# Local attention scores with keys on the partitions, and the softmax sums made across them

## The chip, the cores and the metric

The kernel runs on one core of one Trainium2 chip. The metric is the device time of one execution, in microseconds. Of three timed runs of the kernel before, the median is 2884.61 us, with 2884.58 us as the lowest and 2886.78 us as the highest. The core has five engines that work side by side, each on its own instruction queue in its own order: TensorE (PE, matrix products and transposes; its weight loads are listed apart as PEld), VectorE (DVE), ScalarE (ACT), GpSimd (POOL), and SyncE (SP), which here only issues loads. Matrix products land in a small memory of their own, PSUM; everything else is in SBUF.

## The reference

The input is x of shape (8, 1024, 512) in float32: 8 batches of 1024 tokens. Cut to what matters:

```python
xn = layernorm(x)
q, k, v = split(xn @ local_qkv_w, 3)                      # head size 128
local_out  = softmax(q @ k.T * scale) @ v                 # all 1024 keys
sparse_out = softmax(top-k of (q @ k.T * scale)) @ v      # own weights, k = 102
mem_out    = (softmax(p @ bank.T) @ bank, with p) @ ...   # a memory of 64 rows
pred_out   = two layers with an exact gelu
s = concat(local_out, sparse_out, mem_out, pred_out) @ warboss_w + warboss_b
g = silu(relu(xn @ w1 + b1) @ w2 + b2)                    # 512 -> 2048 -> 512
out = x + s * g
```

The change touches `local_out` alone: the scores of each query against all 1024 keys, the softmax over the keys (largest value subtracted, exponential, division by the sum), and the product with v.

## The kernel before

**Tiling.** A batch has 8 tiles of 128 tokens (`NT`), taken as 4 pairs of 256 tokens (`NP`, `T` = 256). A tile of queries is the unit of the two attentions, a pair is the unit of everything behind them. Over the 8 batches there are 64 tiles and 32 pairs.

**Local attention of one tile** (`local`, line 823). `scores` makes two products of 128 queries by 512 keys, with queries on the partitions, and ACT copies them from PSUM into the tile `el` (128x1024). DVE takes the negated maximum of each row (`nml`, a reduction along the row). ACT forms the exponentials in place with that maximum as its bias and sums them along the row in the same instruction. `normalize` (line 785) takes the reciprocal of the sum on DVE and multiplies the row by it on ACT. `transpose_probs` (line 794) turns the eight 128x128 blocks of probabilities on PE, since the product with v needs the keys on the partitions, and ACT copies the turned blocks to `pT0`. After the second tile of a pair `attend` (line 807) multiplies all 8 chunks of v with `pT0` into the head, 128 channels by 256 queries.

**Sparse attention of one tile** (`sparse`, `sparse_select`) is the same, but its selection takes DVE 13 rounds: eight largest values (MAX8), then their replacement (MATCH_REPLACE8), then the threshold applied in one SCALAR_TENSOR_TENSOR. This is most of DVE's work and is strictly in order.

**The rest.** The feed-forward products, and those of q, k, the memory and the output, are made by a scheme that replaces eight block products by seven and pays with block sums. The sums of PE's results (`add_products`, tiles `u_up`, `u_po`, `m`) and those of its operands (`left_sums`, tile `hs`) are POOL's work; without `hs` PE cannot go on with the second layer of the feed-forward part.

**What sets the order.** Nothing reacts at run time: the program is written out by a planner while it is built. It keeps a clock per engine in units of PE columns (`tick`, `on`, `after`, lines 115 to 128), in which a product of 256 columns counts 256 and a transposition 64. Each piece of work is a generator (a chain) that is put forward again when its due time has come by PE's clock; in between, PE's order is filled with feed-forward products (`feed_forward`, line 665) whenever these are due. `after("dve", 200)` means: go on when DVE should have finished by the planner's price, plus 200 columns. `SLACK` is 400 columns. DVE's rounds of the sparse selection are put into DVE's order whenever DVE's clock falls behind PE's. `pool_is_free` (line 509) holds a POOL instruction back until POOL's planned backlog is under 300 columns. The wrapper `InOrder` (line 79) then fixes each engine's order to the planner's. A new tile is begun every `STEP` columns (line 1076). So the planner's prices decide in which order instructions stand, and on the chip an instruction whose input is late holds up everything behind it on its engine.

All instructions pass through that wrapper, so the profile gives line 85 for almost every one; they are told apart by the names of their tiles.

Of the kernel before, what the change touches and what calls it, by code (L numbers as in the profile page):

```python
# [9 lines left out]
F32 = mybir.dt.float32  # L10
AF = mybir.ActivationFunctionType
ALU = mybir.AluOpType
AX = mybir.AxisListType
PSUM = bass.MemoryType.PSUM

P = 128
# [4 lines left out]
def kernel(  # L21
# [25 lines left out]
    B, S, D = x.shape  # L47
# [4 lines left out]
    NT = S // P  # L52
    NP = NT // 2
    NG = NT // 4
    T = 2 * P
# [3 lines left out]
    NWC = NW // WC  # L59
# [4 lines left out]
    LOCAL, SPARSE = 0, 1  # L64

    const = ctx.enter_context(tc.tile_pool(name="const", bufs=1))
    sb = ctx.enter_context(tc.tile_pool(name="sb", bufs=1))
    small = ctx.enter_context(tc.tile_pool(name="small", bufs=2))
# [8 lines left out]
    class InOrder:  # L77
# [23 lines left out]
    pe, act, dve, pool, sp = (  # L101
        InOrder(e) for e in (nc.tensor, nc.scalar, nc.vector, nc.gpsimd, nc.sync)
    )
# [11 lines left out]
    def tick(columns):  # L115
        clock["pe"] += columns
        while rounds and clock["dve"] < clock["pe"]:
            cost = next(rounds[0], None)
            if cost is None:
                rounds.pop(0)  # L120
            else:
                clock["dve"] = max(clock["dve"], clock["pe"] - 1600) + cost

    def on(engine, columns):
        clock[engine] = max(clock[engine], clock["pe"]) + columns

    def after(engine, more=SLACK):
        return clock[engine] + more
# [29 lines left out]
    def start(generator, due=0, rank=1):  # L158
        chains.append([due, generator, rank])
        chains.sort(key=lambda c: c[2])  # L160

    def matmul(out, lhsT, rhs, start, stop, columns):
        pe.matmul(out, lhsT, rhs, start=start, stop=stop)
        tick(columns)

    def transpose(out, in_, ident):
        pe.transpose(out, in_, ident)
        tick(P // 2)
# [6 lines left out]
    def copy(out, ps, columns):  # L175
        act.copy(out, ps)
        on("act", columns)

    def on_pool(op, out, in0, in1):
        getattr(pool, op)(out, in0, in1)  # L180
        n = 1
        for d in out.shape[1:]:
            n *= d
        on("pool", 60 + int(1.42 * n))
# [5 lines left out]
    def ring(name, shape):  # L190
        return ps_r.tile(list(shape), F32, tag="r", name=name)


    ident = const.tile([P, P], F32, tag="ident", name="ident")
# [35 lines left out]
    for h in range(2):  # L230
        t = sb.tile([P, 2, D], F32, tag="s", name=f"xl_0_{h}", bufs=2)
# [14 lines left out]
    for v in (ffn_b1, mem_out_b, pred_in_b, pred1_b, pred2_b):  # L246
        n = v.shape[0] // P
# [37 lines left out]
    done = set()  # L285
    stats = {}
    xnT = {}
    qT = {}
    kT = {}
    vv = {}  # L290

    def needs(*keys):
        return lambda: all(k in done for k in keys)
# [102 lines left out]
    H = D // 2  # L396
# [376 lines left out]
    probsT = {}  # L773
    heads = {}

    def scores(b, i, h, s):

        for c in range(S // 512):
            ps = ring(f"sc_{b}_{i}_{h}_{c}", (P, 512))
            matmul(  # L780
                ps, qT[b, i // 2][:, h, ts(i % 2, P)], kT[b][:, h, ts(c, 512)], True, True, 512
            )
            copy(s[:, ts(c, 512)], ps, 360)

    def normalize(e, total, name):
        r = small.tile([P, 1], F32, tag="r", name=f"r_{name}", bufs=4)
        dve.reciprocal(r, total)
        on("dve", 100)
        yield after("dve", 100)
        act.activation(e, e, AF.Copy, scale=r)  # L790
        on("act", 690)
        yield after("act")

    def transpose_probs(b, i, h, e):
        if i % 2 == 0:
            if (b, i) != (0, 0):
                yield needs(("head", *divmod(b * NP + i // 2 - 1, NP), h))
            probsT[b, i // 2, h] = sb.tile([P, NT, T], F32, tag=f"pT{h}", name=f"pT_{b}_{i}_{h}")
        for c in range(NT // 4):
            pt = ring(f"ptp_{b}_{i}_{h}_{c}", (P, 4, P))  # L800
            for k in range(4):
                transpose(pt[:, k, :], e[:, ts(4 * c + k, P)], ident)
            copy(probsT[b, i // 2, h][:, ts(c, 4), ts(i % 2, P)], pt, 360)
            yield clock["pe"] + 300
        done.add(("pT", b, i, h))

    def attend(b, p, h):
        ps = ring(f"pa_{b}_{p}_{h}", (P, T))
        accumulate(
            ps,  # L810
            [vv[b][:, k, h, :] for k in range(NT)],
            [probsT[b, p, h][:, k, :] for k in range(NT)],
            T,
        )
        o = sb.tile([P, T], F32, tag=f"head{h}", name=f"head_{b}_{p}_{h}")
        copy(o, ps, 220)
        heads[b, p, h] = o
        done.add(("head", b, p, h))

    def before_pair(b, p):  # L820
        return [] if (b, p) == (0, 0) else [("joined", *divmod(b * NP + p - 1, NP))]

    def local(b, i):
        yield needs(("q", b, i // 2), *[("k", b, g, LOCAL) for g in range(NG)])
        yield after("act", 0)
        if (b, i) != (0, 0):
            yield needs(("pT", *divmod(b * NT + i - 1, NT), LOCAL))
        e = sb.tile([P, S], F32, tag="el", name=f"el_{b}_{i}")
        scores(b, i, LOCAL, e)
        done.add(("local scores", b, i))  # L830
        yield after("act")
        nm = small.tile([P, 1], F32, tag="nm", name=f"nml_{b}_{i}", bufs=4)
        dve.tensor_reduce(nm, e, AX.X, ALU.max, negate=True)
        on("dve", 740)
        yield after("dve", 100)
        total = small.tile([P, 1], F32, tag="total", name=f"totl_{b}_{i}", bufs=4)
        act.activation(e, e, AF.Exp, bias=nm, accum_out=total)
        on("act", 800)
        yield after("act", 100)
        yield from normalize(e, total, f"l_{b}_{i}")  # L840
        yield from transpose_probs(b, i, LOCAL, e)
        if i % 2:
            yield needs(("v", b), *before_pair(b, i // 2))
            yield after("act")
            attend(b, i // 2, LOCAL)
        done.add(("local", b, i))

    def sparse_scores(b, i):
        s = sb.tile([P, S], F32, tag="s", name=f"s_{b}_{i}", bufs=2)
# [38 lines left out]
    def sparse(b, i):  # L888
        n = b * NT + i
        yield needs(("q", b, i // 2), *[("k", b, g, SPARSE) for g in range(NG)])  # L890
        if n > 1:
            yield needs(("chosen", n - 2))
        yield max(clock["pe"], clock["act"]) + (SLACK if n else 100)
        s = sparse_scores(b, i)
        done.add(("sparse scores", n))
        yield after("act")
        o = {}
        rounds.append(sparse_select(b, i, s, o))
        yield lambda: "nm" in o
        if n:  # L900
            yield needs(("pT", *divmod(n - 1, NT), SPARSE))
        e = sb.tile([P, S], F32, tag="es", name=f"es_{b}_{i}")
        act.activation(e, s, AF.Exp, bias=o["nm"])
        on("act", 700)
        o["e"] = e
        yield lambda: "total" in o
        done.add(("chosen", n))
        yield after("dve", 100)
        yield from normalize(e, o["total"], f"s_{b}_{i}")
        yield from transpose_probs(b, i, SPARSE, e)  # L910
        if i % 2:
            yield needs(("v", b), *before_pair(b, i // 2))
            yield after("act")
            attend(b, i // 2, SPARSE)


    def tmp(name):
# [93 lines left out]
    def prepare_stats(b):  # L1011
        yield needs(("xnT", b - 1, NT - 1))
        for j in range(NT):
            t = load_x("xs", b, j)
            yield clock["pe"] + AHEAD // 2
            ln_stats(b, j, t)
            yield clock["pe"] + STEP // 6
        ln_rstd(b, 0, NT)
# [54 lines left out]
            elif p == 2:  # L1073
                form_chunk(0)

    STEP = int(0.995 * (11775 + NWC * (2 * 7 * T + 2 * 7 * H) // 4))
    start(first_tokens())
    start(sparse(0, 0))
    run(needs(("sparse scores", 0)))
# [7 lines left out]
    for n in range(B * NT):  # L1087
        b, i = divmod(n, NT)
        p = i // 2
        now = begin + n * STEP  # L1090
        run(lambda: clock["pe"] >= now)
        start(local(b, i))
        if i == 0:
            start(project_values(b), now + 1000)
            if b + 1 < B:
                start(prepare_stats(b + 1), now + (2000 if b else STEP))
        if i == 3 and b + 1 < B:
            start(prepare_tokens(b + 1))
        if i % 2:
            def two_heads(b=b, p=p):  # L1100
                yield needs(("m", b, p), *before_pair(b, p))
                yield after("act")
                t = starts.pop((b, p))
                yield from prediction_head(b, p, t[:, 1])
                yield from memory_head(b, p, t[:, 0])
                start(finish_pair(b, p), rank=2)

            start(two_heads(), now + 1500)
        if n + 1 < B * NT:
            start(sparse(*divmod(n + 1, NT)), now + int(0.6 * STEP))  # L1110
    run(needs(("out", B - 1, NP - 1)))
# [34 lines left out]
```

## Time and profile before

The profiled execution took 2885.6 us, of which 2883.6 us are the span from its first to its last instruction.

| engine | busy, us | share of the span | instructions |
|---|---|---|---|
| PE | 2844.9 | 99% | 13312 |
| PEld | 2397.6 | 83% | 13312 |
| DVE | 2381.0 | 83% | 3206 |
| POOL | 2184.2 | 76% | 2904 |
| ACT | 1674.4 | 58% | 3175 |

The granted clock of TensorE was 0.997 of full speed. The DMA engines moved 538.90 MB, 187 GB/s on average. Matrix products of float32 stand as two records each, a transposition as one. How to read the rows below: "out<-in" names the tiles written and read, then the operands' shape; in the groups the columns are the total busy time and the mean time of one instruction in ns, then the engine's idle time just before. In the order of time, the columns are start, duration, engine, instruction. Ends of matrix products are modelled and overlap the next start, so PE's pace is read from start to start.

### The profile page before, as it was taken

The page shows a single profiled execution, that of the slowest core. Times are in us where ns is not written, and L with a number is a line of the kernel's source. Part 1 is how long each engine was busy: PE and PEld are TensorE (multiplying, and loading weights), DVE is VectorE, ACT ScalarE, POOL GpSimd, SP SyncE. Part 2 cuts the span into 40 slices and gives each one's busy share as a digit, 9 for nine tenths or more (in the row PEclk, how much of TensorE's full clock was granted, in tenths as well). Part 3 has the DMA queues.
Part 4 walks back from the last instruction along what each step waited for, and adds up shares of the span by engine and source line. Part 5 has one row for each costly group of instructions (what it writes and reads, how often), then busy time and mean ns, then how long its engine had stood idle before and what let it go on. Part 6 is the DMA issues. An engine that isn't in the chain of part 4 may idle for free. (4 is left out here: it accounts for less than half of the span.)

```text
span 2883.6 us, 38540 instructions
## 1 busy us (share of the span) xinstructions
PE 2844.9 (99%) x13312; PEld 2397.6 (83%) x13312; DVE 2381.0 (83%) x3206; ACT 1674.4 (58%) x3175; POOL 2184.2 (76%) x2904
## 2 busy tenths in 40 slices
PE   8989999999999999999999999999999999999998
PEld 6868888888888888888888888888888888888887
DVE  7999878887698787998869987699867989689786
ACT  4546556565565654666546665566655566556564
POOL 3787876878678685786968768688695887868885
PEclk9999999999999999999999999999999999999999
DMA  5665544655446454564545545455455554545545
GB/s 180 218 234 200 209 160 157 218 188 206 147 173 223 167 207 160 180 215 166 208 164 193 209 155 197 165 196 209 153 194 171 205 196 168 190 162 176 198 162 194
DMA packets 132002, 538.90 MB, mean 187 GB/s; under 512 B 13790, under 2 KB 40432, under 8 KB 131808
## 3 DMA queue, kind: packets, MB, share of 16 engines
q1 hardware_dynamic: 126352, 519.23, 51.9%
q0 software_dynamic: 5456, 17.22, 1.6%
q8 instruction: 106, 1.74, 0.2%
q14 instruction: 88, 0.72, 0.1%
HBM read 500.35 MB, written 36.04 MB: 186 GB/s over the span
## 5 line engine op out<-in xcount | busy, mean ns | idle before, releaser
L85 DVE MAX8 top<-left 128x8 f32<-128x1024 f32 x768 | 943.0, 1228 | 26.6
L85 DVE MATCH_REPLACE8 left<-top,left 128x1024 f32<-128x1024 f32 x704 | 850.5, 1208 | 0.0
L85 POOL TENSOR_TENSOR u_up<-u_up 128x256 f32<-128x256 f32 (+1 forms) x640 | 620.1, 975 | 295.2 <-ACT u_up L85 270.9
L85 PE MATMUL f<-w_down,hs 128*128 128x256 f32 x2048 | 537.6, 380 | 0.0
L85 PE MATMUL ph_up<-t,w_up 128*128 128x256 f32 x2048 | 483.3, 380 | 0.8 <-ACT u_up L85 0.8
L85 PEld LDWEIGHTS ph_up<-t,w_up 128*128 128x128 f32 x2048 | 385.2, 191 | 60.5 <-issue 10.2
L85 PEld LDWEIGHTS f<-w_down,hs 128*128 128x128 f32 x2048 | 384.4, 191 | 60.3 <-issue 9.6
L85 PE MATMUL f<-w_down,h 128*128 128x256 f32 x1536 | 424.2, 380 | 6.2 <-ACT h L85 5.8
L85 ACT COPY u_up<-ph_up 128x512 f32<-128x512 f32 (+1 forms) x512 | 265.7, 530 | 236.2 <-PE ph_up L85 234.5
L85 PE MATMUL ph_up<-xnT,w_up 128*128 128x256 f32 x1536 | 382.6, 379 | 0.0
L85 POOL TENSOR_TENSOR hs<-h 128x128 f32<-128x128 f32 x512 | 244.2, 477 | 180.2 <-PE f L85 149.8
L85 PEld LDWEIGHTS f<-w_down,h 128*128 128x128 f32 x1536 | 287.0, 191 | 54.0 <-issue 10.5
L85 PEld LDWEIGHTS ph_up<-xnT,w_up 128*128 128x128 f32 x1536 | 287.7, 190 | 45.6 <-issue 9.3
L85 DVE MAX8 top<-s 128x8 f32<-128x1024 f32 x64 | 78.3, 1224 | 240.2 <-ACT s L85 240.2
L85 PE MATMUL sc<-kT,qT 128*128 128x512 f32 x512 | 240.6, 593 | 0.9 <-ACT u_po L85 0.9
L85 PE MATMUL pa<-pT,v 128*128 128x256 f32 x1024 | 231.6, 379 | 0.0
L85 ACT ACTIVATE h<-u_up,biasT 128x256 f32<-128x256 f32 x512 | 219.6, 501 | 12.2 <-POOL u_up L85 12.2
L85 PEld LDWEIGHTS pa<-pT,v 128*128 128x128 f32 x1024 | 194.3, 190 | 27.6 <-issue 1.4
L85 ACT COPY pT<-ptp 128x512 f32<-128x512 f32 x256 | 148.6, 587 | 114.1 <-PE ptp L85 113.6
L85 DVE TENSOR_REDUCE nml<-el 128x1 f32<-128x1024 f32 x64 | 77.2, 1206 | 134.8 <-ACT el L85 134.6
L85 ACT ACT_TABLE_LOAD x138 | 177.1, 1283 | 4.8 <-DVE nms L85 1.8
L85 POOL TENSOR_TENSOR u_po<-u_po 128x256 f32<-128x256 f32 (+1 forms) x155 | 147.4, 958 | 19.4 <-ACT u_po L85 12.9
(153 smaller groups left out, 4568.5 us busy)
## 6 DMA issues: line engine op xcount, KB each, us to landing
w_down<-w_down_dram SPq DMA_DIRECT2D x248, 896.0 KB, 4.7
w_up<-w_up_dram SPq DMA_DIRECT2D x120, 896.0 KB, 4.6
w_po<-w_po_dram SPq DMA_DIRECT2D x62, 896.0 KB, 4.6
xl<-in_L_attn_x_dram SPq DMA_DIRECT2D x64, 256.0 KB, 4.7
xr<-in_L_attn_x_dram SPq DMA_DIRECT2D x64, 256.0 KB, 5.0
out_dram<-xr POOLq DMA_DIRECT2D x62, 256.0 KB, 2.9
xs<-in_L_attn_x_dram SPq DMA_DIRECT2D x56, 256.0 KB, 4.9
w_q<-w_q_dram SPq DMA_DIRECT2D x15, 896.0 KB, 4.6
```

The lines of the kernel that those rows point to most:

```text
L85: r = made(*args, **kwargs)
```

## The change

The local attention is now made for a pair of tiles at once, with the keys on the partitions. For each of the 8 chunks of 128 keys PE multiplies the chunk of k with the pair's 256 queries; ACT copies the scores to `pT0`, in the order in which the product with v needs them, so the probabilities are not transposed any more.

The maximum over the keys is now over chunks and partitions. `fold` reduces the 8 chunks to one by three DVE operations on contiguous halves (4 chunks against 4, then 2 against 2, then 1 against 1). `across` then reduces over the partitions: two transpositions on PE, a row reduction on DVE (reading PSUM), a copy by ACT that repeats the 2 values of each partition 128 times, two transpositions back, and a copy from PSUM by ACT. That gives a 128x256 tile that holds the negated maximum of each query in all partitions. POOL adds it to the scores in four instructions, and ACT forms the exponentials in two.

The sum over the keys goes the same way (`fold` with additions, then `across` with a reciprocal); for the first four pairs (`EARLY`) the three additions of the fold are POOL's. The probabilities stay undivided: `attend` is made with them, and POOL multiplies the head by the reciprocal sums. `STEP` has a new count of columns, 256 fewer, and the factor 1.0 in place of 0.995.

```diff
--- before.py
+++ after.py
@@ -815,35 +815,96 @@
         o = sb.tile([P, T], F32, tag=f"head{h}", name=f"head_{b}_{p}_{h}")
         copy(o, ps, 220)
         heads[b, p, h] = o
-        done.add(("head", b, p, h))
+        return o
 
     def before_pair(b, p):
         return [] if (b, p) == (0, 0) else [("joined", *divmod(b * NP + p - 1, NP))]
 
-    def local(b, i):
-        yield needs(("q", b, i // 2), *[("k", b, g, LOCAL) for g in range(NG)])
+    def across(ps_name, part, work, op, negate, name):
+
+
+        pt = ring(f"{ps_name}a_{name}", (P, 2, P))
+        for j in range(2):
+            transpose(pt[:, j], part[:, ts(j, P)], ident)
+        of = small.tile([P, 2], F32, tag="of", name=f"of{ps_name}_{name}")
+        dve.tensor_reduce(of, pt, AX.X, op, negate=negate)
+        if not negate:
+            dve.reciprocal(of, of)
+        on("dve", 330)
+        yield after("dve", 200)
+        act.copy(work[:, 2].rearrange("p (j t) -> p j t", j=2), of.unsqueeze(2).to_broadcast([P, 2, P]))
+        on("act", 220)
+        yield after("act", 200)
+        pt = ring(f"{ps_name}b_{name}", (P, 2, P))
+        for j in range(2):
+            transpose(pt[:, j], work[:, 2, ts(j, P)], ident)
+        copy(work[:, 3], pt.rearrange("p j t -> p (j t)"), 220)
+
+    def fold(op, e, work):
+        op(work, e[:, :4], e[:, 4:])
+        op(work[:, :2], work[:, :2], work[:, 2:])
+        op(work[:, 0], work[:, 0], work[:, 1])
+        on("dve", 1400)
+
+    def local(b, p):
+
+
+        n = b * NP + p
+        name = f"{b}_{p}"
+        yield needs(("q", b, p), *[("k", b, g, LOCAL) for g in range(NG)])
         yield after("act", 0)
-        if (b, i) != (0, 0):
-            yield needs(("pT", *divmod(b * NT + i - 1, NT), LOCAL))
-        e = sb.tile([P, S], F32, tag="el", name=f"el_{b}_{i}")
-        scores(b, i, LOCAL, e)
-        done.add(("local scores", b, i))
+        if n:
+            yield needs(("head", *divmod(n - 1, NP), LOCAL))
+        e = sb.tile([P, NT, T], F32, tag="pT0", name=f"pT_{name}_0")
+        probsT[b, p, LOCAL] = e
+        for c in range(0, NT, 2):
+            ps = ring(f"sl_{name}_{c}", (P, 2, T))
+            for u in range(2):
+                matmul(
+                    ps[:, u], kT[b][:, LOCAL, ts(c + u, P)], qT[b, p][:, LOCAL], True, True, T
+                )
+            copy(e[:, c : c + 2], ps, 360)
+        for j in range(2):
+            done.add(("local scores", b, 2 * p + j))
         yield after("act")
-        nm = small.tile([P, 1], F32, tag="nm", name=f"nml_{b}_{i}", bufs=4)
-        dve.tensor_reduce(nm, e, AX.X, ALU.max, negate=True)
-        on("dve", 740)
-        yield after("dve", 100)
-        total = small.tile([P, 1], F32, tag="total", name=f"totl_{b}_{i}", bufs=4)
-        act.activation(e, e, AF.Exp, bias=nm, accum_out=total)
-        on("act", 800)
+        work = sb.tile([P, 4, T], F32, tag="el", name=f"el_{name}")
+        fold(dve.tensor_max, e, work)
+        yield after("dve", 200)
+        yield from across("pm", work[:, 0], work, ALU.max, True, name)
+        yield after("act", 200)
+        for c in range(0, NT, 2):
+            yield pool_is_free
+            on_pool(
+                "tensor_add", e[:, c : c + 2], e[:, c : c + 2],
+                work[:, 3].unsqueeze(1).to_broadcast([P, 2, T]),
+            )
+        yield after("pool", 100)
+        for c in range(0, NT, 4):
+            act.activation(e[:, c : c + 4], e[:, c : c + 4], AF.Exp)
+            on("act", 800 - 100 * (c > 0))
         yield after("act", 100)
-        yield from normalize(e, total, f"l_{b}_{i}")
-        yield from transpose_probs(b, i, LOCAL, e)
-        if i % 2:
-            yield needs(("v", b), *before_pair(b, i // 2))
-            yield after("act")
-            attend(b, i // 2, LOCAL)
-        done.add(("local", b, i))
+        if n < EARLY:
+            yield pool_is_free
+            on_pool("tensor_add", work, e[:, :4], e[:, 4:])
+            yield pool_is_free
+            on_pool("tensor_add", work[:, :2], work[:, :2], work[:, 2:])
+            yield pool_is_free
+            on_pool("tensor_add", work[:, 0], work[:, 0], work[:, 1])
+            yield after("pool", 100)
+        else:
+            fold(dve.tensor_add, e, work)
+            yield after("dve", 200)
+        yield from across("pt", work[:, 0], work, ALU.add, False, name)
+        yield needs(("v", b), *before_pair(b, p))
+        yield after("act")
+        o = attend(b, p, LOCAL)
+        yield after("act", 0)
+        yield pool_is_free
+        on_pool("tensor_mul", o, o, work[:, 3])
+        yield after("pool", 0)
+        done.add(("head", b, p, LOCAL))
+
+    EARLY = 4
 
     def sparse_scores(b, i):
         s = sb.tile([P, S], F32, tag="s", name=f"s_{b}_{i}", bufs=2)
@@ -912,6 +973,7 @@
             yield needs(("v", b), *before_pair(b, i // 2))
             yield after("act")
             attend(b, i // 2, SPARSE)
+            done.add(("head", b, i // 2, SPARSE))
 
 
     def tmp(name):
@@ -1073,7 +1135,7 @@
             elif p == 2:
                 form_chunk(0)
 
-    STEP = int(0.995 * (11775 + NWC * (2 * 7 * T + 2 * 7 * H) // 4))
+    STEP = int(1.0 * (11519 + NWC * (2 * 7 * T + 2 * 7 * H) // 4))
     start(first_tokens())
     start(sparse(0, 0))
     run(needs(("sparse scores", 0)))
@@ -1089,7 +1151,8 @@
         p = i // 2
         now = begin + n * STEP
         run(lambda: clock["pe"] >= now)
-        start(local(b, i))
+        if i % 2 == 0:
+            start(local(b, p))
         if i == 0:
             start(project_values(b), now + 1000)
             if b + 1 < B:
```

## The prediction

> **What bounds the kernel now.** I read the page's first part first, then PE's own waits, then stretches of the timeline, then the groups.
>
> ```profile
> PE 2844.9 (99%) x13312; PEld 2397.6 (83%) x13312; DVE 2381.0 (83%) x3206; ACT 1674.4 (58%) x3175; POOL 2184.2 (76%) x2904
> ```
>
> PE is the bound. Its ends are modelled, so "99%" alone proves little; its waits do:
>
> ```profile
> engine line waited for: us in total, times, longest us
> PE ptx L85 <- DVE xl L85: 8.7, 3, 7.8
> PE f L85 <- ACT h L85: 5.8, 2, 4.7
> PE pk L85 <- ACT xnT L85: 3.0, 3, 1.4
> PE ptp L85 <- ACT es L85: 2.8, 3, 2.1
> ...
> ```
>
> All named waits of PE together are 29.8 us, a good part of them in the start. So the written-out order keeps PE fed although DVE is 83% and POOL 76% busy, and whatever leaves or joins PE's stream counts in full. PE's pace, from the end of the run:
>
> ```profile
> 2817.18 1.88 PE L85 MATMUL sc<-kT,qT 128*128 128x512 f32 x4
> 2818.90 1.89 PE L85 MATMUL ph_po<-w_po,head 128*128 128x256 f32 x8
> 2820.63 1.89 PE L85 MATMUL ph_po<-w_po,ho 128*128 128x256 f32 x8
> ...
> 2844.38 0.60 PE L85 MATMUL ptp<-ident,el 128*128 128x128 f32 x4
> 2844.81 0.60 PE L85 MATMUL f<-w_down,h 128*128 128x256 f32 x2
> ...
> 2857.99 0.60 PE L85 MATMUL ptp<-ident,es 128*128 128x128 f32 x4
> ```
>
> Start to start: four 512-column passes in 1.72 us (430 ns each), eight 256-column passes in 1.73 us (216 ns), four transpositions in 0.43 us (108 ns). A product of 256 columns is two passes, 0.43 us, so a planner's column is worth 1.68 ns.
>
> **PE: what goes.** A pair had 16 transpositions of local probabilities; it now has 8 (four in each `across`): 8 x 108 ns = 0.86 us, times 32 pairs = 27.7 us. The scores cost the same: 8 passes of 430 ns before, 16 of 216 ns after. `attend` is unchanged. PE's stream shrinks by 27.7 us (1.0%), all of it on the path that sets the end. To gain it, PE must not wait more than before.
>
> **ACT.** Per pair go four copies of turned probabilities (587 ns), two divisions of a row (1153 ns) and two reads of the accumulator (189 ns); two broadcast copies (about 407 ns, as the 128x256 `qT` row) and two copies from PSUM (374 ns) come. That is 5.0 us less and 1.6 us more, -3.5 us, 111 us in all. ACT was at 58% and ends no wait of PE that matters, so I count nothing. Its table loads fall from 138 to 136 in the built program: 2.6 us of ACT, nothing.
>
> **DVE: the folds.** Two row maxima of 1206 ns and two reciprocals of 149 ns go (2.7 us per pair). Each fold is three operations with two SBUF operands, of 1024, 512 and 256 elements. Nearest rows:
>
> ```profile
> L85 DVE SCALAR_TENSOR_TENSOR es<-s,top,es x64: 1265/1428/2381, 80.5 to 2853.7; 128x1024 f32<-128x1024 f32 x64
> ```
> ```profile
> L85 DVE TENSOR_TENSOR u_po<-u_po 128x512 f32<-128x512 f32 x2 | 1.4, 692 | 0.6 <-ACT u_po L85 0.6
> ```
> ```profile
> 21.83 3.01 DVE L85 TENSOR_TENSOR w_up<-w_up 128x256 f32<-128x256 f32 x8
> ...
> 53.18 4.62 DVE L85 TENSOR_TENSOR w_m<-w_m 128x256 f32<-128x256 f32 x4
> ```
> ```profile
> 53.09 4.43 POOL L85 TENSOR_TENSOR u_up<-u_up 128x512 f32<-128x512 f32 x4 [1.21 <-ACT u_up L85]
> ```
>
> Free of others the fold is 1.27 (the shortest of 64 SCALAR_TENSOR_TENSOR) + 0.69 + 0.38 (3.01/8) = 2.33 us, and the planner's price for it is 1400 columns, 2.35 us. But see the third and fourth fence: the same 256-element operation takes 0.38 us when POOL is idle, and 1.16 us (4.62/4) at 53 us, where POOL's four instructions fill the same stretch. The Trainium skill ("SBUF — State Buffer", section "Who interferes with whom") speaks against the change here: a DVE instruction with two SBUF inputs and a GpSimd instruction that reads SBUF exclude each other for a whole instruction. The old `nml` reduction had one input and ran at 1206 ns beside a busy POOL; the trace agrees with the rule on both kinds. By the uncontended rows the fold is as planned, 2.33 us. By the rule, with POOL busy over 80% of the time, the first operation waits as the SCALAR_TENSOR_TENSOR does (mean 1586 less 1265 = 0.32 us) and each following one lets one POOL instruction pass: between 0.19 us (mean of all `w_up`, 611, less 418 when free) and 0.78 us (`w_m`); I take 0.5. Fold: 2.33 + 0.32 + 1.0 = 3.65 us, with bounds 2.33 and 5.0 us (2.33 + 1.12 + 2 x 0.78). Without the rule the run would be about 2865 us; with it, as below.
>
> DVE's load: per pair +2 folds (4.7 to 7.3), +2 row reductions of 256 elements (0.41 us each, on the line through 128 elements at 273 ns and 1024 at 1206) and a reciprocal, less 2.7: +3.0 to +5.6 us, some 95 to 180 us in all. DVE goes to 86 to 89%: not the bound, but fuller.
>
> **POOL.** Per pair four additions of 512 elements (1292 ns, the `u_up` row with the same kind of operand) and one product of 256 (764 ns) come, 5.9 us, 190 us in all; the first four pairs' folds add 4 x 4.6 = 18 us. While DVE holds a fold (2.33 us) a busy POOL stands still: 60 folds x 2.33 x 0.8 = 112 us that the planner does not price. POOL goes from 2184 to about 2500 us, 87%. Queued behind a late POOL instruction are `hs` (PE's second layer) and `u_up` (ACT's relu, then buffers for PE).
>
> **Waits that come.** Each pair gets four meetings in which PE itself waits: the first transpositions of `across` behind a fold, the second behind DVE's reduction and ACT's copy, twice. Behind them on PE stands everything. After the maximum's fold the margin is 200 columns (0.34 us) plus what DVE is ahead of plan. That lead can be read at the last tile: the reciprocal of the sum ends at 2855.17, the plan allows 100+690+400 columns (2.0 us) to the transpositions, and they start 2.82 us after, without a wait: 0.8 us ahead, with the SCALAR_TENSOR_TENSOR at its shortest; 0.5 at its mean. So 1.30 us of lateness meets 0.84 us of margin: 0.46 us of wait at the mean fold, and since short folds give nothing back, I take 0.6. After the sum's fold the margin is larger: exponentials priced at 1500 columns (2.52 us) take 2 x 1152 ns = 2.30, and 100 columns stand behind them: 1.23 us, so I take 0.3 us. Together 32 x 0.6 + 28 x 0.3 = 27.6 us (bounds 0 and about 75, where every fold takes 4.4 us or more). For the other 64 meetings, which have 2.6 to 9.5 us of PE work in front of them in the new order against some 2 to 3 us of chain, 3 us; for `hs` and `u_up` coming late from a fuller POOL, 5 us (0 to 45).
>
> The new `STEP` is 125 columns shorter (0.21 us), 13.5 us over 64 tiles; it moves where chains stand. Loads and their queues are unchanged.
>
> **Sum.** 2883.6 - 27.7 + 27.6 + 3 + 5 = 2891.5 us of span. The profiled run has 2.0 us around its span and the median lies 1.0 us above the span, so 2892.5 us, +0.3%.
>
> **Rivals.** (1) Gain kept, faster: folds find POOL between instructions or DVE further ahead; waits add 8 us: 2884.6 - 27.7 + 8 = 2865. For it: 99% busy PE in an order full of such meetings; PE's waits for `es`, behind a DVE instruction that POOL also blocks, are 2.8 us in all. Against: those have three times the margin. (2) The pace decides: tiles begin at `STEP`, and the last tile's chain (sparse scores at 2817.18, its transpositions at 2857.99) ends the run; then the gain is the pace's 13.5 us, 2871. Against: work of others fills PE to its last product. (3) POOL becomes the bound: once its backlog passes the three `hs` that may be made ahead, PE runs at POOL's speed in the stretches with both layers; this decides from about 95% of POOL in such stretches, and costs 0.5 us per tile more or less, 32 us and my 8 us of gain lost besides: about 2930. For it: 87% on average and bursts of four 1.29 us additions. Against: POOL idles 700 us now.
>
> **How the numbers follow.** Main case 0.50, rival (1) 0.22, (2) 0.10, (3) 0.18. The main case's own range is 2875 to 2908 (fold waits of 10 to 43 us), so it lends 0.04 to faster and 0.12 to within 0.2%, which is what a measurement of this kernel tells from no change. Faster: 0.22 + 0.08 + 0.04 = 0.34. Same: 0.12 + 0.02 = 0.14. Slower: 0.34 + 0.18 = 0.52. The range leaves out the better half of (1) and the worse half of (3), a tenth each: 2863 to 2926.
>
> **What would show it.** PE: 256 fewer transpositions and busy time near 2817. The folds' three rows under the tile `el` on DVE: 1.6, 1.2 and 0.9 us if the lock holds, 1.2, 0.7 and 0.4 if not. New rows "pma <- DVE el" and "pta <- DVE el" in PE's waits, 20 to 35 us together. POOL at 85 to 88%. The prediction is wrong if those waits are under 10 us (then 2865), or if PE waits for `hs` or for ACT behind `u_up` by tens of us (then rival 3).

## The result

The changed kernel takes 2906.45 us, median of five runs (2905.11 to 2907.32), against 2886.78 us for the kernel before in the same runs: a ratio of 1.007, 95% interval 1.0059 to 1.0081. It is slower by 0.7%. The forecast was slower, by 0.3%, with a range of 2863 to 2926 us: the side and the range hold, the size was less than half of what came.

The page of the profile after, span and first part:

```profile
span 2905.1 us, 38896 instructions
...
PE 2834.8 (98%) x13312; PEld 2427.3 (84%) x13312; DVE 2533.3 (87%) x3354; ACT 1568.6 (54%) x3045; POOL 2433.4 (84%) x3076
```

DVE has gained 152 us and POOL 249 us of busy time, ACT has lost 106 us. PE's busy time fell by only 10 us though 256 transpositions left it. PE's waits by name, after:

```profile
engine line waited for: us in total, times, longest us
PE pta L85 <- DVE el L85: 12.3, 8, 5.2
PE ptx L85 <- DVE xl L85: 7.9, 1, 7.9
PE pma L85 <- DVE el L85: 7.4, 6, 2.7
PE f L85 <- POOL hs L85: 4.7, 2, 3.6
PE ph_up L85 <- ACT u_up L85: 4.4, 1, 4.4
PE pta L85 <- POOL el L85: 4.0, 2, 3.2
...
```

The first, third and sixth line are new: they are the transpositions of `across` behind a fold (`pma` after the maximum's, `pta` after the sum's; the sixth line is the sum's fold of the first four pairs, which POOL makes). Their counts matter. Of 64 meetings of this kind only 16 are in these lines, and single ones cost up to 5.2 us.

For the balance I took PE's starts from both traces, gave each pass the usual interval to the next start (216 ns for 256 columns, 429 for 512, 109 for a transposition), and split what is over this into waiting and passes at half clock:

| us | before | after | change |
|---|---|---|---|
| PE's passes at the usual pace | 2831.7 | 2804.6 | -27.1 |
| waiting | 29.7 | 67.2 | +37.5 |
| passes at half clock | 5.0 | 15.4 | +10.4 |
| sum | | | +20.8 |
| span | 2883.6 | 2905.1 | +21.5 |

So the saving came in full and was paid back almost twice. The waiting behind the folds went from nothing to 26.9 us (18.5 before `pta`, of which 4.0 by name are behind POOL's folds of the first four pairs; 8.4 before `pma`). The rest of the added waiting, some 10 us, stands mostly before feed-forward products, in a few waits near the start. The half clock can be seen in stretches of both runs. The last columns are the granted clock, the DMA share and GB/s. Before:

```profile
100.00:450.00 350.00, 340.00 (x1579) 284.37 (x1579) 309.83 (x423) 194.38 (x372) 267.87 (x360) 0.99 0.60 208
450.00:2650.00 2200.00, 2190.68 (x10289) 1850.63 (x10288) 1813.16 (x2416) 1306.62 (x2477) 1696.52 (x2235) 1.00 0.53 184
```

After:

```profile
100.00:450.00 350.00, 323.77 (x1468) 272.02 (x1467) 311.91 (x415) 168.22 (x332) 299.29 (x377) 0.96 0.57 196
450.00:2650.00 2200.00, 2181.43 (x10333) 1876.35 (x10332) 1928.96 (x2535) 1229.77 (x2389) 1873.66 (x2359) 1.00 0.53 185
```

The columns after the length are PE, PEld, DVE, ACT, POOL. Much of the loss lies between 100 and 450 us, where PE did 111 fewer passes in the same time and its clock fell from 0.99 to 0.96; by the account above some 18 of the added 37.5 us of waiting stand there.

**One meeting, seen closely.** The worst wait behind a fold, in order of time, PE, then DVE, then POOL, then the last of the two exponentials on ACT, all of the kernel after:

```profile
2312.96 1.89 PE L85 MATMUL ph_po<-w_po,head 128*128 128x256 f32 x8
2320.06 0.66 PE L85 MATMUL pta<-ident,el 128*128 128x128 f32 x2 [5.21 <-DVE el L85]
2320.51 3.62 PE L85 MATMUL ph_po<-w_po,ho 128*128 128x256 f32 x8
2323.92 0.56 PE L85 MATMUL ph_po<-w_po,head 128*128 128x256 f32 x1
```
```profile
2313.51 1.23 DVE L85 MAX8 top<-left 128x8 f32<-128x1024 f32 x1
2314.65 1.68 DVE L85 TENSOR_TENSOR el<-pT 128x1024 f32<-128x1024 f32 x1
2316.36 3.55 DVE L85 TENSOR_TENSOR el<-el 128x512 f32<-128x512 f32 x2
2319.83 0.08 DVE L85 MATCH_VALUE_LOAD left<-top,left 128x8 f32 x1
```
```profile
2313.98 1.26 POOL L85 TENSOR_TENSOR o<-o,m 128x512 f32<-128x512 f32 x1
2315.21 2.25 POOL L85 TENSOR_TENSOR xr<-xr,o 128x512 f32<-128x512 f32 x1
2317.75 0.58 POOL L85 DMA_DIRECT2D out_dram<-xr  x1 [0.30 <-POOL xr L85]
2318.34 1.27 POOL L85 TENSOR_TENSOR xr<-xr,o 128x512 f32<-128x512 f32 x1
```
```profile
2309.86 1.04 ACT L85 ACTIVATE pT<-pT 128x1024 f32<-128x1024 f32 x1
```

Two things come together. The exponentials ended at 2310.90, but DVE, busy with the sparse selection, took up the fold only at 2314.65. And the fold then ran until 2319.83, 5.2 us: its second and third operation took 3.55 us where the shortest of the run take 1.1, while POOL's addition from 2315.21 took 2.25 us where the next took 1.27. PE stands still for 5.2 us. Then the eight passes from 2320.51 take 3.41 us to the next start, 426 ns each in place of 216: the records of the granted clock show half speed for 6.8 us from 2317.5 on. This wait is paid a second time.

The folds' rows after, and the row of POOL's additions:

```profile
L85 DVE TENSOR_TENSOR el<-pT 128x1024 f32<-128x1024 f32 x60 | 91.1, 1518 | 63.5 <-ACT pT L85 58.4 <-POOL o L85 4.6 <-POOL t L85 0.3
L85 DVE TENSOR_TENSOR el<-el 128x512 f32<-128x512 f32 x60 | 58.6, 977 | 2.1
L85 DVE TENSOR_TENSOR el<-el 128x256 f32<-128x256 f32 x60 | 45.7, 761 | 2.1
L85 POOL TENSOR_TENSOR pT<-pT,el 128x512 f32<-128x512 f32 x128 | 167.7, 1330 | 52.0 <-ACT el L85 52.0
```

A fold takes 1.52 + 0.98 + 0.76 = 3.26 us in the mean, against an estimate of 2.33 us free of POOL (the shortest of each row add up to 1.21 + 0.69 + 0.42 = 2.32) and a price of 2.35 us.

### The profile page after: what moved, and what is told of

It reads as the page before. It is cut to its first block, busy times and chain, and to the rows that moved or that the text cites. A ratio compares the mean times of both kernels' runs of the same rounds, so it can differ in the third digit from the quotient of the medians.

```text
span 2905.1 us, 38896 instructions
## 1 busy us (share of the span) xinstructions
PE 2834.8 (98%) x13312; PEld 2427.3 (84%) x13312; DVE 2533.3 (87%) x3354; ACT 1568.6 (54%) x3045; POOL 2433.4 (84%) x3076
## 5 line engine op out<-in xcount | busy, mean ns | idle before, releaser
L85 POOL TENSOR_TENSOR u_up<-u_up 128x256 f32<-128x256 f32 (+1 forms) x640 | 627.7, 986 | 165.6 <-ACT u_up L85 140.9
L85 POOL TENSOR_TENSOR hs<-h 128x128 f32<-128x128 f32 x512 | 254.7, 498 | 97.0 <-PE f L85 88.4
L85 POOL TENSOR_TENSOR pT<-pT,el 128x512 f32<-128x512 f32 x128 | 167.7, 1330 | 52.0 <-ACT el L85 52.0
L85 POOL TENSOR_TENSOR u_po<-u_po 128x256 f32<-128x256 f32 (+1 forms) x155 | 150.3, 975 | 11.2 <-ACT u_po L85 4.8
L85 POOL TENSOR_TENSOR m<-m 128x256 f32<-128x256 f32 (+1 forms) x155 | 150.6, 975 | 10.5 <-ACT m L85 6.0
L85 DVE BATCH_NORM_STATS2 st<-xs 128x6 f32<-128x512 f32 x56 | 38.0, 679 | 126.6 <-DMA xs<-in_L_attn_x_dram 126.6
L85 DVE TENSOR_TENSOR el<-pT 128x1024 f32<-128x1024 f32 x60 | 91.1, 1518 | 63.5 <-ACT pT L85 58.4
```

The lines of the kernel that those rows point to most:

```text
L85: r = made(*args, **kwargs)
```

## The experiments

Two theories stood at first. A: folds that POOL lengthens hold up PE. B: POOL is too full and late with its own sums. The kernel before ran at 2885.4 to 2886.6 us (medians) beside all of them.

### Folds with one operand: 2905.3 us

```diff
-        op(work, e[:, :4], e[:, 4:])
-        op(work[:, :2], work[:, :2], work[:, 2:])
-        op(work[:, 0], work[:, 0], work[:, 1])
+        dve.tensor_reduce(work[:, 0], e.rearrange("p c t -> p t c"), AX.X, op)
```

> Each fold is one DVE reduction over a strided view of all 8 chunks (2048 elements, one SBUF operand) in place of three operations with two SBUF operands; the planner's price stays 1400 columns, so every engine's order is that of the changed kernel. Theory A (folds that wait for POOL hold up PE): the fold takes about 2.3 us whatever POOL does, the waits of PE for DVE's tile el (12.3 + 7.4 us by name) fall under 6 us, half-speed clock goes with them, and the time falls by 20 to 30 us, to 2876 to 2886 us. Theory B (a fuller POOL is late with its sums): the time falls by under 8 us, to 2898 us or more. If a strided read costs more than 1 ns an element, the fold is slower than before and A expects the waits to grow.

Measured: 2905.31 us (ratio to before 1.0067, 1.0052 to 1.0082), no change. The fold's row tells why the test did not separate the theories:

```profile
L85 DVE TENSOR_REDUCE el<-pT x60: 3641/3740/3819, 51.3 to 2844.3; 128x256 f32<-128x2048 f32 x60
```

Least, median and greatest lie within 5%, so POOL does not touch it, but the strided reading costs 1.8 ns an element and the fold takes 3.74 us, longer than the three operations. The waits stayed (`pta` 14.2, `pma` 5.6 us by name). Two things can be read from it. POOL, with the same instructions, fell from 2433 to 2382 us:

```profile
PE 2832.8 (98%) x13312; PEld 2422.7 (83%) x13312; DVE 2552.0 (88%) x3234; ACT 1569.5 (54%) x3045; POOL 2381.6 (82%) x3076
```

Only the folds differ, so the 52 us are what their second operand had cost POOL. And a fold that POOL does not lengthen, but that is 0.5 us longer by itself, costs the same 2905 us: the loss needs a late fold, whatever makes it late. The run is also a base with the changed kernel's order in which only the fold's length need be changed.

### The fold at its measured price: 2920.9 us

```diff
-        on("dve", 1400)
+        on("dve", 1950)
```

> The changed kernel with the fold priced at 1950 columns (3.28 us, what its three instructions took in the profile) in place of 1400. Theory A (the fold is late against the written-out order because the price leaves the waiting for POOL out): PE work is put in front of the transpositions behind a fold, the waits for el fall by about two thirds, and the time falls by 12 to 22 us, to 2884 to 2894 us. Theory B (POOL's load): under 5 us of change.

Measured: 2920.92 us (1.0122, 1.0107 to 1.0137), 14 us slower than the changed kernel, where 12 to 22 us faster was expected. The waits for `el` did fall, as A says, to 3.9 us by name; but others came. By the same account as above the waiting is 76.4 us in all, with 12.3 before `ph_up`'s products with `t`, 12.3 before those with `hs` and 9.9 before the token transpositions (more still stands before the transpositions of the sparse probabilities, whose wait for `es` went from 1.3 to 8.5 us by name), and 21.7 us go at half clock. With this price the wait was not planned away: put elsewhere in the order, it was paid elsewhere. No other price was tried.

### Without POOL's additions: 2866.7 us

```diff
-        for c in range(0, NT, 2):
-            yield pool_is_free
-            on_pool(
-                "tensor_add", e[:, c : c + 2], e[:, c : c + 2],
-                work[:, 3].unsqueeze(1).to_broadcast([P, 2, T]),
-            )
-        yield after("pool", 100)
...
-            act.activation(e[:, c : c + 4], e[:, c : c + 4], AF.Exp)
+            act.activation(e[:, c : c + 4], e[:, c : c + 4], AF.Exp, scale=0.01)
```

> Leaves out POOL's four additions of the negated maximum per pair (168 us of POOL in all); the exponential takes the scores times 0.01 instead, so the output is another one. The maximum is still formed. Theory B (POOL's load costs PE): POOL falls to about 2270 us, PE's waits for hs, h and u_up go back to what they were before the change, the time falls by 15 to 25 us, to 2882 to 2892 us. Theory A (folds against POOL): the folds stay, a little less blocked because POOL is 78% instead of 84% busy; the time falls by 3 to 10 us, to 2896 to 2904 us.

Measured: 2866.70 us (0.9934, 0.9917 to 0.9951), 40 us less than the changed kernel, more than B expected and far more than A. PE's passes are the same 2804.2 us, the waiting is 34.9 us and the half clock 8.5 us. In the middle of the run PE is as good as never late:

```profile
450.00:2650.00 2200.00, 2197.96 (x10438) 1892.74 (x10437) 1924.44 (x2576) 1232.57 (x2400) 1786.16 (x2291) 1.00 0.53 188
```

So the 27 us of the transpositions are a real gain, which shows where nothing takes it back. But this run leaves out POOL's work and also the place where the chain waits for it.

### The pace as before: 2909.4 us

```diff
-    STEP = int(1.0 * (11519 + NWC * (2 * 7 * T + 2 * 7 * H) // 4))
+    STEP = int(0.995 * (11519 + NWC * (2 * 7 * T + 2 * 7 * H) // 4))
```

> The changed kernel with the factor of STEP at 0.995, as it was before the change. Theory C (the pace of the tiles ends the run): tiles begin 129 columns (0.22 us) sooner, 14 us over 64 tiles, and the time falls by 8 to 14 us. Theories A and B: the tiles begin sooner but DVE and POOL have no more time, so the time stays within 5 us of 2906 or grows by up to 10 us.

Measured: 2909.43 us (1.0083, 1.0068 to 1.0098). Tiles that begin sooner gain nothing; the rival in which the pace decides is out.

### Folds half as long, all else kept: 2874.8 us

The base is the run with one operand (2905.3 us).

```diff
-        dve.tensor_reduce(work[:, 0], e.rearrange("p c t -> p t c"), AX.X, op)
+        dve.tensor_reduce(work[:, 0], e[:, :4].rearrange("p c t -> p t c"), AX.X, op)
```

> The kernel with one reduction per fold, over four of the eight chunks only: leaves out the maximum and the sum over the other four, so the output is another one. One SBUF operand, 1024 elements, about 1.9 us (the reduction over eight took 3.74 us and gave 2905 us). Order and prices stay those of the changed kernel, POOL keeps its load. Theory A (PE waits where a fold takes longer than about 3.5 us): the waits of PE for DVE's el, 14.2 and 5.6 us there, fall to under 4 us, half-speed clock falls with them, time 2876 to 2886 us. Theory B (POOL's load): DVE's shorter folds do not help POOL; 2897 to 2905 us.

Measured: 2874.76 us (0.996, 0.9946 to 0.9974). Against the base, with order, prices and POOL's work unchanged, 30.5 us go with 1.8 us of each of 60 folds. The fold's row and PE's waits:

```profile
L85 DVE TENSOR_REDUCE el<-pT x60: 1907/1950/1981, 50.0 to 2819.2; 128x256 f32<-128x1024 f32 x60
```

```profile
PE pta L85 <- POOL el L85: 5.0, 2, 4.2
PE ph_up L85 <- ACT u_up L85: 4.4, 1, 4.4
PE f L85 <- POOL hs L85: 4.3, 2, 4.1
PE pta L85 <- DVE el L85: 3.1, 3, 1.7
```

The waits for DVE's `el` have fallen from 19.8 to 4.0 us (3.1 before `pta`, 0.9 before `pma`), those for POOL are where they were. This is what theory A said; the time fell a little further than its 2876 to 2886 us.

### POOL's additions beside the chain: 2903.0 us

```diff
+    def load_pool(b, p):
+        for c in range(0, NT, 2):
+            yield pool_is_free
+            v = b2.rearrange("p (c n) -> p c n", n=P - M)
+            on_pool("tensor_add", v, v, bankT[:, M:].unsqueeze(1).to_broadcast([P, D // (P - M), P - M]))
...
         yield from across("pm", work[:, 0], work, ALU.max, True, name)
+        start(load_pool(b, p))
```

> As the run without POOL's additions (2866.7 us), but POOL makes four additions of 512 elements per pair all the same, on a constant tile (zero is added), in a chain that nothing waits for; leaves out the subtraction of the maximum, exponential of the scores times 0.01, another output. Theory B (POOL's time is what costs): 2890 us or more, as the changed kernel has. Theory D (it is the place of the additions between the two folds, where the exponentials and the second fold wait for them): 2866 to 2876 us.

Measured: 2903.00 us (1.0058, 1.0043 to 1.0073). Against the run without additions 36 of the 40 us are back, though nothing waits for these additions. So it is POOL's time, not the additions' place, that costs. PE's waits for DVE's `el`, which had gone, are back with 12.8 us by name (8.7 and 4.1), and those for `xl` went from 9.0 to 14.4. Part of how it costs is in the folds, which became longer: 1285 + 879 + 656 = 2.82 us without the additions, and here

```profile
L85 DVE TENSOR_TENSOR el<-pT 128x1024 f32<-128x1024 f32 x60 | 89.7, 1495 | 111.5 <-ACT pT L85 93.4 <-POOL m L85 18.0
L85 DVE TENSOR_TENSOR el<-el 128x512 f32<-128x512 f32 x60 | 65.2, 1087 | 2.1
L85 DVE TENSOR_TENSOR el<-el 128x256 f32<-128x256 f32 x60 | 44.1, 736 | 2.1
```

3.32 us. The planner also holds POOL's other sums back for the new ones, so the order differs from that of the run before; how much each of the two does is open.

### The same POOL load on the kernel before: 2897.6 us

The same `load_pool`, started at each second tile of the old `local`.

> The kernel before with four POOL additions of 512 elements per pair on a constant tile (zero is added; the output is the reference's) in a chain that nothing waits for, about 165 us of POOL more, to some 2350 us. Theory B: it gets slower by 15 us or more, to 2902 us and up. Theory D or A: under 8 us slower, 2887 to 2895 us.

Measured: 2897.55 us (1.0039, 1.0024 to 1.0054): 11.0 us slower, between both expectations. POOL stands at 2338.5 us there. The same 128 additions cost 11 us where no fold exists and 36 us where folds do. Neither theory alone gives this: folds and additions together cost more than the sum of their parts. Two engines that hold each other up would do that. But POOL and DVE are also fuller in the run with folds (84% and 87%, against 81% and 82%), and that alone could do it; no run tells the two apart.

### DVE's time given back elsewhere: 2887.7 us

```diff
             dve.reciprocal(of, of)
+        dve.tensor_reduce(work[:, 1, :3], b2.unsqueeze(1).to_broadcast([P, 3, D]), AX.X, ALU.max)
```

> The run with folds over four chunks (2874.8 us; leaves out the other four, another output) with one more DVE reduction of a constant tile, 1536 elements and about 1.75 us, behind each walk's reduction, where PE waits for nothing: DVE gets back the 1.8 us per fold that the short folds saved, at another place. Theory A1 (what costs is the fold's length, at the place where PE waits): 2872 to 2882 us. Theory A2 (what costs is DVE's whole time, wherever it stands): 2895 to 2908 us.

Measured: 2887.65 us (1.0008, 0.9998 to 1.0017), on the base with short folds, between both expectations. DVE is back at 2540 us, and 12.9 of the 30.5 us are back with it. PE waits at other places instead; these two lines were 7.8 and 1.5 us with the short folds alone:

```profile
PE ptx L85 <- DVE xl L85: 10.8, 7, 7.8
PE ptp L85 <- ACT es L85: 8.6, 6, 3.2
```

So of what the long fold costs, 12.9 us are DVE's time at this other place, and the remaining 17.6 us are put down to the fold's standing in front of a meeting with PE.

### Shifts from fewer chunks: 2892.6 and 2892.0 us

```diff
-        fold(dve.tensor_max, e, work)
+        dve.tensor_max(work[:, :2], e[:, :2], e[:, 2:4])
+        dve.tensor_max(work[:, 0], work[:, 0], work[:, 1])
+        on("dve", 1400)
```

> The changed kernel, but the shift of the softmax is the maximum over the first four of the eight chunks (two operations, of 512 and 256 elements, in place of three): any shift near the maximum gives the same softmax. The sum is over all chunks. Prices and orders are those of the changed kernel. Theory A1: the waits behind the first fold (7.4 us by name) go, the second fold's stay: 2890 to 2898 us. Theory A2: DVE is 46 us fuller by less, about 40% of what the short folds saved: 2892 to 2898 us as well. Theory B (POOL's time alone): 2900 us or more.

> The changed kernel with the shift of the softmax taken from the first of the eight chunks alone, so that the first fold has no operation left; its price stays in the plan, so the order is that of the changed kernel. The sum is over all chunks. In these inputs the largest score of a query lies up to 71 above the largest of its first chunk, which an exponential in float32 still bears (it ends at 88); with other inputs it might not. All folds on DVE of the first kind gone: 104 us of DVE, against 46 us in the run with half of the chunks, which gave 2892.6 us. The waits behind the second fold (about 11 us by name) should stay. If time goes on falling with DVE's load at the rate of that run (14 us for 44 us, most of it waits behind the first fold that are gone already there), no further than to 2884 to 2890 us; by the rate of DVE's time alone (12.9 us for 111 us) 2884 to 2887 us.

Measured: 2892.59 us with half of the chunks (1.0027, 1.0017 to 1.0037), 2891.96 us with one (1.0023, 1.0014 to 1.0032). Half the chunks do it: `pma`'s waits for `el` fell from 7.4 to 1.2 us, 14 us are saved, and leaving out the rest of the fold, though DVE falls from 2489 to 2432 us, saves nothing that can be told, where 2884 to 2890 us was expected. What remains stands behind the sum's fold, 11.2 and 11.9 us by name. Neither beats the kernel before.

### The sum by a product with ones: 2920.3 us

```diff
-        yield from across("pt", work[:, 0], work, ALU.add, False, name)
+        pt = ring(f"pts_{name}", (P, T))
+        matmul(pt, ones.to_broadcast([P, P]), work[:, 0], True, True, T)
+        dve.reciprocal(work[:, 3], pt)
+        on("dve", 250)
...
+            dve.tensor_mul(o, ps, by)
```

> The changed kernel with its second walk across the partitions replaced by one product with ones (the sum stands in all partitions at once), the reciprocal taken by DVE from PSUM, and the head multiplied by it by DVE from PSUM in place of ACT's copy and POOL's product. Per pair PE saves nothing (4 transpositions for 2 passes), POOL saves 0.76 us, and one meeting of PE with DVE and ACT goes. Theory A: the wait behind the second fold stays, 2896 to 2906 us. Theory B: 24 us of POOL go, worth 3 to 6 us: 2899 to 2903 us. Below 2886 us it would beat both kernels, which no theory expects.

Measured: 2920.30 us (1.0116, 1.0101 to 1.0131), 14 us slower than the changed kernel, against all expectations. The reciprocal of 128x256 took 1742 ns in the median, on a price of 250 columns (0.42 us); DVE rose to 2569 us, and PE waited 22.4 us by name for the fold in front of the product. A meeting less on PE did not help: the wait at the remaining one grew.

### Early sums on DVE: 2923.1 us

`EARLY` from 4 to 0.

> The changed kernel with the first four sums folded by DVE as all others are (EARLY 0). POOL's three additions there take 4.4 us of its time each. If the start, where 19 us more are lost between 100 and 450 us than before the change, is lost to POOL, the time falls by 3 to 10 us; if to DVE, which is behind with its selections there, it grows by 3 to 10 us.

Measured: 2923.13 us (1.0131, 1.0116 to 1.0146), 17 us slower, where 3 to 10 us were expected if DVE lacks time at the start. PE's waits for DVE's `el` before `pta` rose from 12.3 to 19.9 us. This points to DVE. But the new prices move the order of the whole run, and the loss is not all at the start, so it cannot be put down to the four folds alone.

## Why the prediction was right in its side and short in its size

**PE's saving**: 27.7 us foretold, 27.1 measured. The step holds. That PE's busy time would fall to 2817 us was wrong (2834.8): busy time also holds the passes at half clock, 10.4 us more than before.

**Where the size was lost.** The forecast had 27.7 us of saving against 35.6 us of waits, +7.9. Measured are 27.1 us of saving, 37.5 us of added waits and 10.4 us of passes at half clock, +20.8. So 10.4 of the 13 us between them are a term that the forecast put at nothing, the clock, and some 2 us are waits. That the waits agree so well is in part luck, as shown below.

**ACT**: -111 us foretold, -106 measured, worth nothing, as said.

**The fold's length**: 3.65 us foretold from the rows of the kernel before, 3.26 measured, between the bounds of 2.33 and 5.0. The weighing of rule against row was right: with the rule left out, the forecast would have been a fold of 2.33 us and a time of 2865 us. That POOL and DVE hold each other up is now shown from both sides: DVE's two-operand rows are longer beside POOL than their shortest, and POOL is busy 52 us less when the folds have one operand. The step had POOL standing 112 us, and at 2500 us in all; it came to 2433.

**Waits behind the folds**: 27.6 us foretold, 26.9 measured. But the terms of that sum do not agree. The step took 0.6 us for each first fold and 0.3 us for each second on DVE, 19 and 8 us; measured are 8.4 us behind the first and 18.5 us behind the second, 4.0 of these by name behind POOL's own folds of the first four pairs, for which no wait was foretold. Most folds made nobody wait (the plan had up to 5 us left there). Some 17 did, most of them of 3.5 us and more, and their waits were up to 5.4 us each; but some folds as long made nobody wait. A mean lateness against a mean margin was the wrong sum to make; it is the tail that costs. The margin of 1.23 us behind the second fold was no margin where DVE itself came late. The three longest waits behind DVE's second folds (5.4, 2.8 and 2.7 us by the starts, at 2320, 2849 and 728 us) all come after folds that DVE took up 2.6 to 3.7 us after the exponentials had ended.

**POOL's load**: 5 us foretold, as late sums for PE. As such it came out about right: with the 3 us for other meetings it makes 8, where some 10 were measured, 4.7 of them by name for `hs`. What the step missed is that POOL's load does not end there. The additions cost 36 us by the pair of runs with and without them; these are no cost besides the balance, but stand in its waits and its half clock. POOL's time and the folds are not two terms: take away the additions, or half of the fold's elements, and 30 us or more go.

**The clock**: no step had it. A wait that lowers the clock costs again: 10.4 us more of passes at half clock than before. With this term the forecast would have been 2903.

**The rivals.** (1), the gain kept, is what the runs with short folds or without additions show, 2875 and 2867 us; in the kernel as it is it did not come. (2), the pace, fell with the run at 0.995. (3), POOL as the bound, did not come as described: POOL is at 84%, and PE waits 4.7 us for `hs`. Its sum also counts 8 us of gain that the main sum does not have; 8 us of loss and 32 us give 2925, not 2930.

**The signs.** PE's waits for DVE's `el` are 19.7 us by name, at the edge of the 20 to 35 foretold, and POOL's 84% lies just under the 85 to 88%.

What stays open: how the 36 us of POOL's additions divide between longer folds, POOL's own lateness and the planner's moved order. No run has folds of one operand without the additions, so it is not shown how much of this needs DVE and POOL to hold each other up.

## What to carry to other kernels

Work that is taken off a full engine is a gain only if what replaces it does not end in front of that engine; a chain that goes PE, DVE, PE, ACT, PE in a fixed order makes the full engine wait for the tail of the others' times, not for their means. Operations on DVE with two operands from SBUF and a busy POOL take time from each other, here 0.9 us of each fold of 2.3 us and 52 us of POOL's 2433: their loads should not be priced apart. And a wait should be priced with what the clock may take after it.

## What the runs showed of the hardware that was not expected

- **The clock after a wait.** The wait of 5.21 us at 2320 us was followed by eight passes of 426 ns in place of 216. The records of the granted clock show half speed for 13.7 us of the working span before and 37.5 us after, in pieces of 3.4 us and their multiples. The Trainium skill ("TensorE: Matmul & The Clock Gate", section "Part 1: The HAM clock gate") says that the clock falls to half after one or more idle windows of about 3.4 us. The pieces here have that length, but shorter waits were enough. The wait that ended at 2849.50 us was 2.68 us, and the four passes from 2851.27 took 1.71 us, 427 ns each; in the kernel before, a wait of 2.40 us that ended at 1714.74 was followed by half clock from 1715.2 to 1718.6. A wait of 2.55 us that ended at 727.98 us was not: the ten passes from 728.23 took 2.16 us, 216 ns each. So in these traces the length of a wait alone does not decide.

```profile
2849.50 0.41 PE L85 MATMUL pta<-ident,el 128*128 128x128 f32 x2 [2.68 <-DVE el L85]
2849.75 1.73 PE L85 MATMUL f<-w_down,h 128*128 128x256 f32 x4
2851.27 1.91 PE L85 MATMUL f<-w_down,hs 128*128 128x256 f32 x4
2852.98 0.78 PE L85 MATMUL f<-w_down,h 128*128 128x256 f32 x2
```
```profile
727.98 0.41 PE L85 MATMUL pta<-ident,el 128*128 128x128 f32 x2 [2.55 <-DVE el L85]
728.23 2.33 PE L85 MATMUL ph_k<-t_k,w_k 128*128 128x256 f32 x10
730.39 1.03 PE L85 MATMUL ph_k<-xnT,w_k 128*128 128x256 f32 x4
```

- **Strided reading on DVE.** A reduction over 2048 elements with a stride of 256 elements took 3740 ns, 1.8 ns an element, and over 1024 elements 1950 ns, 1.9 ns an element; the contiguous row maximum of 1024 elements took 1206 ns before.
- **The reciprocal.** One of 256 elements in each partition, read from PSUM, took 1742 ns, 6.8 ns an element; the reciprocals of one or two elements, at some 150 ns, had not let this be seen.
